# Second pass of a graph kernel: TensorE's results staged by ScalarE and added two experts later, self loops made ahead of the gathers, a written order on four engines

## The chip, the core and the metric

The kernel runs on one core of a Trainium2 chip, as one program. The metric is the time of one execution in microseconds (us) on the device; the smaller, the better. Before the change the median of nine runs is 2969.44 us, and the runs lie between 2944.95 and 2984.15 us.

The core's engines run side by side, each with its own queue, and wait for each other through semaphores. TensorE (PE) multiplies matrices and writes into PSUM, a small memory in banks of 512 floats per partition. VectorE (DVE) and ScalarE (ACT) read PSUM and the larger on-chip memory, SBUF. GpSimd (POOL) issues the indirect transfers here, and SyncE (SP) most of the direct ones.

## The reference

Two layers over 3125 nodes with 256 features and 103125 edges (50000 random pairs in both directions, and a self loop for each node). Cut to what matters:

```
xn = layernorm(x)
x  = x + L0_gnn(xn, src, dst) + L0_mix(xn)             # a maximum over edges, and attention
x  = x + L0_ffn(layernorm(x))                          # two experts for all nodes
xn = layernorm(x)
x  = x + L1_gnn(xn, src, dst, edge_type) + L1_mix(xn)  # a sum over edges by relation, and attention
x  = x + L1_ffn(layernorm(x))                          # eight experts, two weighted by node
```

The change lies in the second layer:

```
# L1_gnn
agg  = segment_sum((xn @ W[r])[src, edge_type], dst)
h    = gelu(agg + xn @ loop_w + h_bias + xn)
gnn  = layernorm(h) * ln_gamma + ln_beta
# L1_ffn, xn now the normalised x
w    = softmax over the two largest of xn @ Wr + br, 0 for the other six experts
y    = sum over e of w[e] * (gelu(xn @ W1[e] + b1[e]) @ W2[e] + b2[e])
```

All eight experts are computed for every node, since the weights differ from node to node.

## The kernel before

Nodes are sorted by the number of their edges and put into 25 tiles of 128 (the last has 53). A tile `t` of the second pass needs `STEPS[t]` gathers: each one fetches, for the 128 nodes, one row of 256 floats of the table `htab` in device memory (`gather`, L193). `edge_pass` (L1334) walks over groups of tiles (`GROUPS1`: first the four tiles 15 to 18, whose gathers start early, then 23 and 24, 19 to 22, 12 to 14, 9 to 11, 7 and 8, 5 and 6, 3 and 4, and 2, 1, 0 alone). Up to four gathers fill one of five `gt` buffers, and VectorE adds them up (L1356) and into the tile's accumulator (L1361), which begins as the row of the tile's self-loop edge.

Everything else of the layer is background work. It stands as a list of jobs with a cost in `bg`. After each buffer of gathers, `edge_pass` takes as many jobs from the list as a credit allows: 0.9 to 1.3 units of cost for each gather, as is left in the list against the gathers left in the group. So the jobs are written between the gather sums, and VectorE and POOL execute them in this written order (`manual_schedule` with these two engines). TensorE and ScalarE get their order from the planner of the language, which sorts by its own estimate of costs. On the chip each engine then runs its queue strictly in the order decided at build time.

When the last tile of a group has its sums, `after1` appends that group's jobs (class `Group`, L2286), which run beside the gathers of the next group:

- `sums_a`, `sums_b`, `sums_c`: TensorE makes the products of the nodes' own rows with `w_lu`, a matrix of two halves (`loop_w` plus the identity, and the attention's matrix), into PSUM (L2300 to L2302). VectorE adds one half to the accumulator (L2307) and the other to `x` (L2308), and ScalarE applies Gelu (L2309).
- `states_a` to `states_d`: two layer norms on VectorE, with three square roots on ScalarE in between.
- `routes_a`, `routes_b`, `shares`: TensorE transposes the normalised rows and makes the router's logits (L2378); VectorE ranks the experts in `top2` (L197), which has one Exp on ScalarE; TensorE transposes the weights, and ScalarE copies them (L2399).
- ten steps (`step`, L2461). `hidden(e)` makes an expert's first products (L2408) into four PSUM banks, and ScalarE's Gelu moves them to SBUF as `hT` (L2412, three buffers). `outputs(e)` makes the second products (L2439) into two more banks, one bank for two tiles. `take` at the beginning of the next step has VectorE multiply each tile's result by its weight and add it to `x`, straight out of PSUM (L2458). `constants` does the same for the biases `b2` (L2425, L2450, L2456).

The last four steps of a group (`late`) are put between the first jobs of the next one. A finished tile is scattered to the output by POOL (L240), nine buffers of gathers after its last step. Before all this the list holds the attention: `att_k`, `att_softmax`, then `att_ctx` (L2241) for each tile, and `att_end`.

Of the kernel before, what the change touches and what calls it, by code (L numbers as in the profile page):

```python
# [32 lines left out]
NX = 8  # L33
# [27 lines left out]
SECONDS = 5  # L61

# [27 lines left out]
def rows(t):  # L90
    return LAST if t == NT - 1 else P
# [9 lines left out]
def gps_kernel(ctx: ExitStack, tc: tile.TileContext, a, out):  # L101
# [1216 lines left out]
    def fast():  # L1318
        fx = ExitStack()
# [245 lines left out]
        with ExitStack() as l0x:  # L1565
# [376 lines left out]
            ET = mybir.EngineType  # L1942
# [216 lines left out]
        with ExitStack() as l1x:  # L2159
# [23 lines left out]
            f1 = l1x.enter_context(tc.tile_pool(name="f1", bufs=3))  # L2183
# [57 lines left out]
            def att_ctx(t):  # L2241
                r = rows(t)
                pt = ps_tr.tile([P, 2, P], F32, name="pt")
                PE.transpose(pt[:r, 0, :], kT[:, t * P : t * P + r], ident)
                ks = kp.tile([P, P], F32, name="ks1", bufs=3)
                S.activation(ks[:r, :], pt[:r, 0, :], AF.Copy, scale=rs2[:r, t : t + 1])
                PE.matmul(pctx, ks[:r, :], x[:r, t, :], start=(t == 0), stop=(t == NT - 1))  # L2247

            def att_sum():
                S.copy(g_t, pctx)  # L2250
# [35 lines left out]
            class Group:  # L2286


                def __init__(self, tiles, accs):
# [3 lines left out]
                    self.hT, self.ys = {}, []  # L2293

                def loops(self, a, b):

                    for j in range(a, min(b, self.k)):
                        pa = self.pa[j] = ps_mm.tile([P, 512], F32, name="mm")
                        at = slice(self.tiles[j] * P, (self.tiles[j] + 1) * P)
                        PE.matmul(pa, xT[:, 0, at], w_lu[:, 0, :], start=True, stop=False)  # L2300
                        PE.matmul(pa[:, :D], ones_row, b_h, start=False, stop=False, skip_group_check=True)  # L2301
                        PE.matmul(pa, xT[:, 1, at], w_lu[:, 1, :], start=False, stop=True)  # L2302

                def gelus(self, a, b):
                    for j in range(a, min(b, self.k)):
                        t, mg, pa = self.tiles[j], self.accs[j], self.pa.pop(j)
                        V.tensor_tensor(mg, mg, pa[:, :D], op=ALU.add)  # L2307
                        V.tensor_tensor(x[:, t, :], x[:, t, :], pa[:, D:], op=ALU.add)  # L2308
                        S.activation(self.hh[:, j, :], mg, AF.Gelu)  # L2309

                def sums_a(self):
                    self.hh = fin.tile([P, 4, D], F32, name="hh")
                    self.mvh = [small.tile([P, 4, 2], F32, name=f"mvh{i}") for i in range(2)]
                    self.rsh = [small.tile([P, 4], F32, name=f"rsh{i}") for i in range(3)]
                    self.pa = {}
                    self.loops(0, 2)

                def sums_b(self):
                    self.gelus(0, 2)
                    self.loops(2, 4)  # L2320

                def sums_c(self):
                    self.gelus(2, 4)
# [41 lines left out]
                def routes_a(self):  # L2365
# [9 lines left out]
                    self.pl = ps_tr.tile([P, 512], F32, name="pt")  # L2375
                    for j, t in enumerate(self.tiles):
                        for c in range(2):
                            PE.matmul(  # L2378
                                self.pl[:, j * NX : (j + 1) * NX], xT[:, c, t * P : (t + 1) * P], wr1[:, c, :],
                                start=(c == 0), stop=(c == 1),  # L2380
                            )

                def routes_b(self):
                    k = self.k
                    lg1 = fin.tile([P, 4, NX], F32, name="lg1")
                    V.tensor_tensor(
                        lg1[:, :k, :], self.pl[:, : k * NX].rearrange("p (j e) -> p j e", e=NX),
                        br1[:, None, :].to_broadcast([P, k, NX]), op=ALU.add,
                    )
                    w_full, _ = top2(lg1[:, :k, :], k, fin)  # L2390
                    V.tensor_copy(wf[:, self.s, :], w_full)

                def shares(self):
# [6 lines left out]
                    self.constants()  # L2400

                def hidden(self, e):
                    n, at0 = self.n, self.at0
                    hT = self.hT[e] = f1.tile([P, FC, 4 * P], F32, name="hT1")
                    for f in range(FC):
                        ph = ps_mm.tile([P, 512], F32, name="mm")
                        for c in range(2):
                            PE.matmul(  # L2408
                                ph[:, :n], w1s[e][:, c, f * P : (f + 1) * P], xT[:, c, at0 : at0 + n],
                                start=(c == 0), stop=(c == 1),  # L2410
                            )
                        S.activation(hT[:, f, :n], ph[:, :n], AF.Gelu, bias=b1[:, e, f : f + 1])  # L2412

                def bank(self):
                    turn[0] += 1
                    return ps_acc.tile([P, 512], F32, name="py", tag=f"acc{1 + turn[0] % 2}")

                def constants(self):

                    for j0 in range(0, self.k, 2):  # L2420
                        pb = self.bank()
                        two = self.tiles[j0 : j0 + 2]
                        for j, t in enumerate(two):
                            r, at = rows(t), (j0 + j) * P
                            PE.matmul(  # L2425
                                pb[:r, j * D : (j + 1) * D], self.wT[:, at : at + r], b2a, start=True, stop=True
                            )
                        self.ys.append((None, two, pb))

                def outputs(self, e):  # L2430

                    hT = self.hT.pop(e)
# [227 lines left out]
```

## Time and profile before

| what | value |
|---|---|
| median of nine runs | 2969.44 us |
| the profiled execution | 2958.72 us |
| its span | 2957.0 us |
| second pass, from its first gather on | 1652 to 2957 us |
| last sum of gathered rows | 2899 us |
| VectorE's busy time in L2458 | 88.1 us, 200 instructions |
| ScalarE's busy time from 1652 us on | 289 us |
| granted TensorE clock, mean | 0.766 |

A row of the groups' view reads: line, engine, operation, output and inputs by the names in the program, shapes, count, then busy time and the mean of one in ns, and after the bar the time in which the engine stood idle just ahead of these instructions, with what ended the waiting. In the view of waits the three numbers are us in total, how often, and the longest. "issue" is time in which the engine waited for nothing that the profile shows. "remote", or "another core or an unknown queue", marks a wait whose releasing event the profile could not name. A matrix product of 32-bit floats shows as two records.

### The profile page before, as it was taken

Reading aid. Unit: us, or ns where it says so; the run is one execution under the profiler, and the core shown is the slowest. Engines: PE = TensorE matmul, PEld = TensorE weight load, DVE = VectorE, ACT = ScalarE, POOL = GpSimd, SP = SyncE. Lnnn points to the kernel's source line nnn. Section 1 sums busy time; section 2 is a strip of 40 time slices with the busy share of each in tenths; the row PEclk is TensorE's granted clock in tenths of the full one; section 3 lists DMA queues with packets and bytes.
Section 4 is the critical chain, followed back from the end, with each engine's and each line's share of the span. In section 5 each row is a group of like instructions: output and inputs, shape, how many; then the busy total and the mean of one; then the engine's idle time right before and its main releaser. Section 6 shows DMA issues by size and latency. Waiting matters only on the chain.

```text
span 2957.0 us, 20996 instructions
## 1 busy us (share of the span) xinstructions
PE 1878.8 (64%) x6033; PEld 1173.0 (40%) x6033; DVE 1256.5 (42%) x3537; ACT 558.5 (19%) x1275; POOL 1727.2 (58%) x1830
## 2 busy tenths in 40 slices
PE   4374666403473754266798447867887787786877
PEld 3132333202341433134443224554455455564656
DVE  7443444536324434324665334334353344343342
ACT  5122221000110101012221112121112121222234
POOL 5566665676647477646026764665666566665561
PEclk9666877655785766567899667887898788887889
DMA  6433333343323233333256642232332223222220
GB/s 190 127 88 88 92 90 95 94 106 111 94 62 106 61 96 95 90 70 81 74 196 227 213 124 64 84 89 81 88 89 84 80 81 86 82 87 83 77 82 16
DMA packets 125963, 290.09 MB, mean 98 GB/s; under 512 B 41387, under 2 KB 63983, under 8 KB 122633
## 3 DMA queue, kind: packets, MB, share of 16 engines
q0 software_dynamic: 83184, 230.02, 28.2%
q1 hardware_dynamic: 38122, 55.88, 5.6%
q10 hardware_dynamic: 4526, 2.71, 0.3%
q8 instruction: 51, 0.84, 0.1%
q14 instruction: 80, 0.65, 0.1%
HBM read 249.07 MB, written 39.41 MB: 98 GB/s over the span
## 4 chain that ended last, share of the span: by engine, by line
PE 27%; issue 8%; another core or an unknown queue 6%; DVE 5%; POOL 3%; ACT 2%; DMA 1%; DVEq 0%; POOLq 0%; ACTq 0%
PE mm L2408 10%; PE py L2439 8%; PE mm L188 4%; POOL gt L193 3%; DVE gt L1356 1%; PE mm L2302 1%; PE pt L2378 1%; DVE bnst L162 1%; PE mm L2300 1%; ACT hT L2412 0%; PE py L2425 0%; PE mm L2301 0%; PE pctx L2247 0%; DMA gt<-htab_f,idx2g 0%
## 5 line engine op out<-in xcount | busy, mean ns | idle before, releaser
L193 POOL DMA_INDIRECT gt<-btab,idx x814 | 804.9, 989 | 476.1 <-issue 225.9
L193 POOL DMA_INDIRECT gt<-htab_f,idx2g x742 | 732.3, 987 | 463.8 <-DVE acc L1361 227.3
L2408 PE MATMUL mm<-xT,w 128*128 128x256 f32 (+4 forms) x1408 | 438.7, 462 | 125.5 <-issue 78.3
L1356 DVE TENSOR_TENSOR gt<-gt 128x256 f32<-128x256 f32 (+1 forms) x767 | 409.9, 534 | 80.7 <-remote 36.6
L2439 PE MATMUL py<-w,hT 128*128 128x256 f32 (+1 forms) x1600 | 395.8, 401 | 58.5 <-issue 28.9
L2408 PEld LDWEIGHTS mm<-xT,w 128*128 128x128 f32 x1408 | 269.6, 219 | 272.1 <-issue 187.5
L2439 PEld LDWEIGHTS py<-w,hT 128*128 128x128 f32 (+1 forms) x1600 | 314.6, 200 | 130.7 <-issue 73.9
L2458 DVE SCALAR_TENSOR_TENSOR x<-py,wf,x 128x256 f32<-128x256 f32 x200 | 88.1, 478 | 484.9 <-remote 204.5
L2412 ACT ACTIVATE hT<-mm,b 128x256 f32<-128x256 f32 (+4 forms) x352 | 168.3, 496 | 569.7 <-PE mm L2408 251.3
L188 PE MATMUL mm<-w_rel,xT 128*128 128x512 f32 x400 | 178.8, 605 | 6.0 <-ACT xT L183 3.9
L1532 PE MATMUL mm<-w,hT 128*128 128x256 f32 x400 | 131.5, 489 | 68.5 <-issue 47.1
L1503 PE MATMUL mm<-xT,w 128*128 128x384 f32 (+2 forms) x320 | 113.9, 522 | 91.6 <-issue 39.0
L1361 DVE TENSOR_TENSOR acc<-acc,gt 128x256 f32<-128x256 f32 x371 | 158.4, 427 | 27.4 <-DVE gt L1356 11.5
L1532 PEld LDWEIGHTS mm<-w,hT 128*128 128x128 f32 x400 | 94.1, 246 | 120.3 <-issue 77.2
L188 PE MATMUL mm<-w_qkv,xT 128*128 128x512 f32 (+1 forms) x200 | 102.0, 633 | 43.4 <-ACT vs L1751 28.1
L1503 PEld LDWEIGHTS mm<-xT,w 128*128 128x128 f32 x320 | 70.1, 244 | 134.3 <-issue 61.1
L188 PE MATMUL pt<-w_own,xT 128*128 128x256 f32 x100 | 39.8, 527 | 123.2 <-DVE acc L1845 69.1
L188 PEld LDWEIGHTS mm<-w_rel,xT 128*128 128x128 f32 x400 | 76.3, 194 | 100.9 <-issue 88.3
L1863 PE MATMUL pmean<-ones,xt 128*128 128x1 f32 (+1 forms) x100 | 21.0, 314 | 130.0 <-DVE xt L171 86.6
L193 POOL DMA_INDIRECT gt<-htab_f,soon x72 | 72.2, 1003 | 46.3 <-issue 20.0
L1620 DVE COPY slots<-gt 128x4 f32<-128x4 f32 (+1 forms) x214 | 38.5, 180 | 134.9 <-DMA gt<-btab,idx 134.5
L1507 ACT ACTIVATE hT<-mm,b 128x384 f32<-128x384 f32 (+2 forms) x80 | 40.3, 517 | 223.6 <-remote 140.8
(436 smaller groups left out, 2088.2 us busy)
## 6 DMA issues: line engine op xcount, KB each, us to landing
htab_f<-hs SPq DMA_DIRECT2D x25, 1024.0 KB
gt<-btab,idx POOLq DMA_INDIRECT x814
gt<-htab_f,idx2g POOLq DMA_INDIRECT x742
w<-in_f_W_dram SPq DMA_DIRECT2D x20, 512.0 KB
ntab<-x SPq DMA_DIRECT2D x5, 640.0 KB
btab<-bs SPq DMA_DIRECT2D x5, 640.0 KB
x<-in_x_dram SPq DMA_DIRECT2D x4, 640.0 KB
otab<-xn SPq DMA_DIRECT2D x16, 128.0 KB
```

What stands on the lines that cost most here:

```text
L188: PE.matmul(ps, lhs[:, c, t * P : (t + 1) * P], w[:, c, :], start=start and c == 0, stop=stop and c == 1)
L193: G.indirect_dma_start(out=dst, out_offset=None, in_=table, in_offset=bass.IndirectOffsetOnAxis(ap=idx, axis=0))
L1356: V.tensor_tensor(gt[:, :h, :], gt[:, :h, :], gt[:, m - h : m, :], op=op)
L1361: V.tensor_tensor(acc, own(t) if i == 0 else acc, gt[:, 0, :], op=op)
L1503: PE.matmul(ph[:, :n], w1[:, i, c, f * P : (f + 1) * P], xT[:, c, at0 : at0 + n], start=(c == 0), stop=(c == 1),)
L1507: S.activation(hT[:, f, :n], ph[:, :n], AF.Gelu, bias=b1[:, i, f : f + 1])
L1532: PE.matmul(py[:, i * D : (i + 1) * D], hTs[i][:, f, j * P : (j + 1) * P], w2[:, i, f, :], start=False, stop=(f == FC - 1), skip_group_che ...
L1620: V.tensor_copy(slots_of[t][:, U - 1 - k1 : U - 1 - k0], gw[:, : k1 - k0, D])
L2408: PE.matmul(ph[:, :n], w1s[e][:, c, f * P : (f + 1) * P], xT[:, c, at0 : at0 + n], start=(c == 0), stop=(c == 1),)
L2412: S.activation(hT[:, f, :n], ph[:, :n], AF.Gelu, bias=b1[:, e, f : f + 1])
L2439: PE.matmul(py[:r, j * D : (j + 1) * D], hT[:, f, at : at + r], w2s[e][:, f, :], start=(f == 0), stop=(f == FC - 1),)
L2458: V.scalar_tensor_tensor(d, y, wf[:r, t, e : e + 1], d, op0=ALU.mult, op1=ALU.add)
```

## The change

The change touches the second pass, the function `fast`.

1. ScalarE and TensorE join the engines with a written order: all four now run the second pass as the jobs write it. The jobs of a group are interleaved by hand with the end of the group before (`group_jobs`, `last_jobs`).
2. `brought` has ScalarE copy each expert's results out of PSUM into one of two `ys` buffers in SBUF, multiplied by the weight. `taken` has VectorE add a whole group's buffer to `x` in one instruction, and it does so as late as the buffers allow: when both are full and a third result is to be staged, the older one is added first.
3. `loops` makes the products with `w_lu` for the next group two steps ahead of the end of this one's jobs, while that group's gathers are still running, and ScalarE copies both halves to SBUF (`hu`). `sums` then adds from SBUF.
4. The router's logits are copied to SBUF by ScalarE, `hT` has two buffers in place of three, and `att_ctx` makes its product after the next tile's transposes (`att_add`).

```diff
+YS = 2
...
-            f1 = l1x.enter_context(tc.tile_pool(name="f1", bufs=3))
+            f1 = l1x.enter_context(tc.tile_pool(name="f1", bufs=2))
...
-                PE.matmul(pctx, ks[:r, :], x[:r, t, :], start=(t == 0), stop=(t == NT - 1))
+                if t:
+                    att_add(t - 1)
...
+                def loops(self):
+                    self.hu = fin.tile([P, 4, 2, D], F32, name="hu")
+                    self.hh = self.hu[:, :, 0, :]
...
+                    for j, (pa, _) in enumerate(pas):
+                        got = S.copy(self.hu[:, j, :, :], pa.rearrange("p (m d) -> p m d", m=2))
+                def sums(self):
...
+                    for j, mg in enumerate(self.accs):
+                        V.tensor_tensor(self.hh[:, j, :], self.hh[:, j, :], mg, op=ALU.add)
+                        S.activation(self.hh[:, j, :], self.hh[:, j, :], AF.Gelu)
+                    V.tensor_tensor(x[:, self.s, :], x[:, self.s, :], self.hu[:, :k, 1, :], op=ALU.add)
...
+                def brought(self, e):
+                    if len(brought) == YS:
+                        taken()
+                    ys = fin.tile([P, 4, D], F32, name="ys", bufs=YS)
...
+                        if e is None:
+                            got = S.copy(ys[:r, j, :], py)
+                        else:
+                            got = S.activation(ys[:r, j, :], py, AF.Copy, scale=wf[:r, t, e : e + 1])
+                    brought.append((self, e, ys))
...
                 def step(self, i):
-                    self.take()
-                    if i < NX:
-                        self.hidden(i)
-                    if 1 <= i <= NX:
-                        self.outputs(i - 1)
...
+                    self.hidden(i)
+                    self.outputs(i - 1 if i else None)
+                    self.gelus(i)
+                    self.brought(i - 1 if i else None)
+            def taken():
+                group, e, ys = brought.popleft()
...
+                    d = x[:, tiles[0] : tiles[0] + k, :]
+                    V.tensor_tensor(d, d, ys[:, :k, :], op=ALU.add)
...
+            def group_jobs(new, old):
+                k, c = new.k, old.k if old else 0
+                out = [(3.0, new.sums)]
+                if old:
+                    out.append((1.5 * c, all_of(
+                        lambda: old.hidden(6), lambda: old.gelus(6), lambda: old.outputs(5), lambda: old.hidden(7),
+                    )))
+                out += [(1.5, new.states_a), (1.5, new.states_b), (1.0, new.states_c)]
+                if old:
+                    out.append((2.0 * c, all_of(
+                        lambda: old.brought(5), lambda: old.gelus(7), lambda: old.outputs(6),
+                    )))
+                out += [(1.0, new.states_d), (4.0, new.routes_a)]
+                if old:
+                    out.append((2.5 * c, all_of(
+                        lambda: old.brought(6), lambda: old.outputs(7), lambda: old.brought(7),
+                    )))
+                out += [(2.0, new.routes_b), (2.0, new.shares)]
+                out += [((1.6 if i == 0 else 3.1) * k, lambda i=i: new.step(i)) for i in range(6)]
+                return out
...
+                jobs = group_jobs(groups1[g], groups1[g - 1] if g else None)
+                if g + 1 < len(GROUPS1):
+                    groups1.append(Group(GROUPS1[g + 1], None))
+                    jobs.insert(len(jobs) - 2, (2.0, groups1[g + 1].loops))
...
-            with tc.manual_schedule(engines={mybir.EngineType.DVE, mybir.EngineType.Pool}):
+            with tc.manual_schedule(engines={ET.DVE, ET.Pool, ET.PE, ET.Activation}):
                 first_group()
```

## The prediction

> **What bounds the kernel now.** I read the page first. No engine is full: POOL, which issues the gathers, is the busiest over the second pass, and the chain that ended last runs through TensorE's two FFN lines.
>
> ```profile
> PE 1878.8 (64%) x6033; PEld 1173.0 (40%) x6033; DVE 1256.5 (42%) x3537; ACT 558.5 (19%) x1275; POOL 1727.2 (58%) x1830
> PE mm L2408 10%; PE py L2439 8%; PE mm L188 4%; POOL gt L193 3%; DVE gt L1356 1%; PE mm L2302 1%; PE pt L2378 1%; DVE bnst L162 1%; PE mm L2300 1%; ACT hT L2412 0%; PE py L2425 0%; PE mm L2301 0%; PE pctx L2247 0%; DMA gt<-htab_f,idx2g 0%
> ```
>
> Next the waits from 1651 us to the end, which is the second pass. VectorE spends 440 us in three rows in front of one line, L2458, the weighted addition out of PSUM. POOL then waits for VectorE, since its gathers need the five `gt` buffers back.
>
> ```profile
> POOL gt L193 <- DVE acc L1361: 227.3, 53, 13.2
> DVE x L2458 <- remote: 204.5, 15, 24.6
> DVE x L2458 <- PE py L2439: 149.5, 50, 20.1
> DVE x L2458 <- PE mm L2408: 85.7, 8, 25.7
> ```
>
> Third, busy time by group of tiles (columns: window, length, then busy PE, PEld, DVE, ACT, POOL). I cut the windows where the gathers of one group end; the cuts are those of the sum below.
>
> ```profile
> 1652.00:1714.00 62.00, 14.79 (x40) 8.22 (x38) 19.54 (x21) 9.84 (x17) 47.98 (x47) 0.56 0.54 167
> 1714.00:1809.00 95.00, 55.97 (x165) 31.04 (x166) 43.24 (x106) 22.84 (x44) 45.76 (x46) 0.73 0.33 96
> 1809.00:1980.00 171.00, 141.46 (x488) 92.48 (x486) 65.94 (x165) 31.90 (x53) 105.24 (x109) 0.85 0.30 85
> 1980.00:2135.00 155.00, 119.61 (x375) 71.47 (x376) 59.83 (x149) 27.83 (x51) 99.77 (x101) 0.80 0.30 88
> 2135.00:2299.00 164.00, 126.79 (x405) 81.66 (x404) 67.09 (x168) 28.11 (x46) 102.22 (x105) 0.83 0.29 86
> 2299.00:2420.00 121.00, 95.82 (x317) 63.91 (x316) 48.08 (x126) 23.14 (x40) 70.84 (x73) 0.84 0.28 80
> 2420.00:2541.00 121.00, 97.42 (x359) 70.03 (x359) 50.21 (x129) 27.95 (x49) 73.77 (x76) 0.87 0.29 82
> 2541.00:2662.00 121.00, 87.48 (x326) 68.35 (x324) 49.50 (x128) 24.59 (x49) 78.30 (x80) 0.82 0.30 86
> 2662.00:2727.00 65.00, 40.09 (x143) 29.96 (x144) 24.58 (x66) 13.46 (x26) 40.47 (x43) 0.77 0.30 85
> 2727.00:2801.00 74.00, 58.92 (x227) 45.38 (x227) 24.89 (x63) 17.85 (x36) 41.37 (x43) 0.89 0.28 79
> 2801.00:2899.00 98.00, 76.58 (x397) 64.12 (x396) 44.95 (x135) 37.20 (x83) 54.60 (x55) 0.87 0.25 73
> ```
>
> The reader is to see that every stretch is longer than its PE time and longer than its POOL time: the two alternate. The cause is a loop. PSUM has two output banks, four tiles fill both, and VectorE frees them by an addition that stands in its queue among the gather sums. TensorE waits for VectorE to come round, then VectorE waits for TensorE.
>
> Last, the timeline, around one 20 us wait:
>
> ```profile
> 1806.89 7.07 PE L2439 MATMUL py<-w,hT 128*128 128x256 f32 x32
> ...
> 1874.52 4.70 PE L2439 MATMUL py<-w,hT 128*128 128x256 f32 x21
> 1876.62 0.95 POOL L193 DMA_INDIRECT gt<-htab_f,idx2g  x1 [0.30 <-issue]
> 1882.54 1.29 PE L2439 MATMUL py<-w,hT 128*128 128x256 f32 x2 [1.73 <-issue]
> 1885.34 0.58 PE L2439 MATMUL py<-w,hT 128*128 128x256 f32 x1 [1.51 <-issue]
> 1895.31 1.66 DVE L2458 SCALAR_TENSOR_TENSOR x<-py,wf,x 128x256 f32<-128x256 f32 x4 [20.15 <-PE py L2439]
> ```
>
> The same 32 products took 7.07 us at 1807 and 20 us at 1875, with nothing awaited ("issue"). TensorE has slow stretches of its own, and the change doesn't touch them.
>
> **The change part by part.**
>
> *Additions staged (L2412 to L2459).* VectorE loses 200 L2458 instructions at 478 ns (88 us of busy time on the page), 14 of L2450 (8.1) and 2 of L2456 (0.7): 97 us. It gains nine additions for each of eleven groups. Priced by SBUF rows of the same width, 426 ns at 256, 685 at 512, 1.22 us at 1024 and about 0.95 between for 768, a round over all groups is 3 x 0.43 + 4 x 0.69 + 2 x 0.95 + 2 x 1.22 = 8.4 us, so 76, and 4 for the short last tile. 17 us of VectorE saved, beside gathers and off the path. What counts is its 440 us of waiting. An expert's result is now added two steps after it is staged; a four-tile step of TensorE takes 7.0 (L2408 x16) + 7.07 (L2439 x32) = 14 us, so VectorE may run some 28 us ahead before it waits: longer than any single wait above (25.7).
>
> ScalarE gains 200 scaled evictions of 128x256; the nearest row is its own Gelu of that shape, 472 ns (copies without a scale 373): 94 us, plus 25 constants at 373 ns (9). ScalarE then works some 400 us of 1150, and a four-tile step has 4 x 0.69 + 4 x 0.47 = 4.6 us of it under 14 us of TensorE. It is hidden as long as VectorE hands back one of the two `ys` buffers; a late VectorE holds the eviction, the next Gelus queued behind it, and so TensorE.
>
> The Trainium skill ("ScalarE: Activation LUTs", Rules for kernel authors) speaks against this: additions and multiplications belong on VectorE. The rows put the two engines level here, 478 ns against 472; by the rule up to 94 us would come back (2934 in the end), by the trace none, since they lie under TensorE's work.
>
> *Self loops ahead (L2295 to L2309).* TensorE's products stay (50 each of L2300, L2301, L2302). Moved ahead, they take away VectorE's wait at L2307 (55.1 + 4.8 us). ScalarE gains 25 copies of 128x512 at 590 ns (15 us), behind TensorE. VectorE loses 50 PSUM additions at 415 ns (21 us) and gains 25 at 427 plus one wide addition a group: 10.7 + 8.4 = 19. Level.
>
> *`hT` buffers three to two.* Nothing: on a TensorE in program order the products that read a buffer are over before the Gelus that refill it can start.
>
> *`att_ctx`.* The product moves behind the next transposes. Its wait for ScalarE is 14.5 us in all, in stretches where VectorE waits for gathers anyway: between 0 and -14, I take 0.
>
> *Table loads.* ScalarE made 56 in this pass at 1283 ns. The written order needs about four a switch, 43: -17 us of ScalarE, hidden; 0.
>
> *Queues passed.* Expert loads and `otab` loads on SP keep their place among the gathers. Scatters on POOL (1021 ns each) are released by the last addition, two steps later, and POOL's wait for it is bounded by the nine chunks kept in between, so 0; past the last gather nothing is behind them but the end.
>
> *Fixed order on TensorE and ScalarE.* This is the cost. At each of ten group switches: `hidden(0)` of the new group now stands behind the transposes of the routing weights. Before, it ran while VectorE ranked experts (7.79 us from 1789.85, beside ranking from 1790.04 to 1795.3). Transposes and logits wait on VectorE and ScalarE with nothing between, some 2.5 us. And the Exp stands on ScalarE behind the evictions of experts 6 and 7. Lower bound 0 (VectorE's pace by gathers is slower than TensorE anyway), upper bound 7.8 + 2.5 + 7 (one `outputs`) = 17 us a switch. I take 8, nearer the first, since most stretches have TensorE time to spare.
>
> **The sum.** A gather takes 0.95 + 0.30 us when POOL waits for nothing (the row at 1876.62). By stretch the larger of gathers x 1.25 and today's busy PE: 58 (46 gathers), 58 (46), 141 (PE), 120 (PE), 127 (PE), 96 (PE), 97 (PE), 97 (77 gathers), 51 (41), 59 (PE), 77 (PE), and the 58 us tail as it is: 1039 us, where 1305 were spent. That is 266 us to win at most. Back come 10 x 8 = 80 us of switches, and part of TensorE's own delays: VectorE's "remote" waits of 204.5 us were moments in which TensorE's results came late. Bounds 0 (all absorbed by the 28 us of slack) and 204; slack hides them from VectorE but TensorE and ScalarE still pay in the stretches where PE is the larger, so I take 60. Gain 266 - 80 - 60 = 126 us. The profiled execution took 2958.7 us, so 2833; the median of the runs lies 10.7 us above it: about 2843, said as 2840.
>
> The page counts 51 packets of the instruction queue q8 for 12066 PE instructions and weight loads, 16.5 KB and some 237 instructions each. The Trainium skill ("Runtime: NRT & Kernel Launch", Instruction fetch mechanics) says that code comes in 16 KiB blocks of 256 instructions and that crossing one is mostly hidden. By that rule the slow stretch at 1875 would not be the fetch and the 60 us would be 0; the trace shows the slowness, whatever its cause, and the sum goes by it.
>
> **The rivals.**
>
> *All of it is won.* The slack absorbs switches and late results: 2969 - 266 = 2703, with half the switches 2743. For it: 28 us exceeds each wait. Against it: in six stretches TensorE is already the longer side, and it must also meet its partners in order.
>
> *TensorE simply is the bound.* If its "remote" and slow time all comes back (204) together with a switch cost of 6 us, the gain is gone: 2969 - 266 + 204 + 60 = 2967, no change. For it: 1809 to 1980, PE 83% busy with few waits on VectorE. Against it: the 155 us and 164 us stretches with 36 us of idle PE each.
>
> *Slower: the strict order closes a new loop at the switches.* VectorE needs the Exp, the Exp stands behind the evictions of experts 6 and 7, those need `outputs(7)`, which stands behind transposes that need VectorE; gathers stop with VectorE once the five buffers are full. It decides from 27 us a switch (266 / 10); at 32 us the time is 3020. For it: TensorE's lag of up to two steps (28 us) must be worked off just there. Against it: 17 us was the worst I could add up, and one round of the old loop cost 20 to 25 us too.
>
> **How the numbers follow.** Forecast (2780 to 2900): 0.47. All won (2690 to 2780): 0.18. No change, or nearly (2900 to 2985): 0.17, of it 0.07 below 2954. Slower by the loop: 0.18. About 0.5% (15 us) is what a measurement of this kernel can tell from no change. So faster 0.47 + 0.18 + 0.07 = 0.72, same 0.10, slower 0.18. The range leaves out a tenth at each end: 2715 to 3000.
>
> **What will show it.** Right: VectorE's waits on TensorE at the additions fall from 440 us to under 100, POOL's wait for VectorE at L193 from 227 to under 110, second-pass PE idle from about 350 us to 220, ScalarE to about 400 us busy. Wrong: a new top wait, VectorE on ScalarE (the Exp in `top2` or the Sqrt in `root`) above 150 us in all, or TensorE idle above 15 us at each switch. The forecast fails high if TensorE's slow stretches grow as it gets denser, and low if they vanish.

## The result and the profile after

| | before | after |
|---|---|---|
| median of the runs (62 and 20) | 2959.94 us | 3029.97 us |
| ratio after / before, 95% interval | | 1.0206 [1.018, 1.0232] |
| second pass in the profiled execution | 1305 us | 1408 us |
| TensorE busy in it | 958 us | 968 us |
| VectorE waiting in front of the experts' additions | 440 us | 303 us (L2474) |
| all waits of POOL for VectorE in it | 303 us | 397 us |

The changed kernel is 2.1% slower. The ratio leaves out the runs that lie over 1.5% above the fastest of their kernel; the medians of all runs give 2.4%. The readings of "after" are taken from a run of the unaltered changed kernel that was made beside the first experiments (profiled execution: 3057.7 us, 28 above the median; span 3056.0 us, second pass from 1648 us). The page's engine row and its chain by line answer the two shown before:

```profile
PE 1890.0 (62%) x6033; PEld 1183.6 (39%) x6033; DVE 1235.8 (40%) x3415; ACT 649.8 (21%) x1525; POOL 1733.8 (57%) x1830
...
PE mm L2402 11%; PE py L2430 9%; PE mm L190 5%; DVE gt L1359 1%; ACT hT L2412 1%; PE mm L2315 1%; PE mm L2313 1%; ACT ys L2447 1%; PE mm L2214 0%; PE pctx L2256 0%; PE py L2428 0%; DVE bnst L164 0%; PE mm L2314 0%; DVE x L2346 0%
```

The work went where the change puts it: VectorE has 122 instructions less, ScalarE 250 more and 91 us more to do. TensorE's work is the same. The waits of the second pass (us in total, times, longest):

```profile
POOL gt L195 <- DVE acc L1364: 260.9, 34, 38.0
DVE x L2474 <- ACT ys L2447: 230.7, 27, 27.4
...
DVE bnst L164 <- ACT hu L2325: 187.1, 9, 41.6
...
ACT hT L2412 <- remote: 138.0, 29, 10.5
ACT ys L2447 <- remote: 122.9, 10, 26.7
...
DVE x L2474 <- ACT ys L2445: 72.6, 6, 24.6
...
DVE t_w L219 <- ACT t_w L216: 57.5, 7, 21.0
```

VectorE still waits 303 us at the additions (L2474), now for ScalarE's staged results in place of TensorE's PSUM; the whole idle time in front of the line is 392, where it was 485. Two waits stand beside that: 187 us for the Gelu of new sums (L2325; `bnst` is the first operation of the norm behind it), where before has no such row, and 58 us for the ranking's Exp (L216), which was 35. ScalarE itself waits in rows that end in "remote": the product that it needs is over in TensorE's records, and the signal comes later. By group, in the same cut as before (window, length, busy PE, PEld, DVE, ACT, POOL, then granted clock, DMA share, GB/s):

```profile
1813.00:2005.00 192.00, 143.75 (x492) 93.69 (x490) 62.66 (x139) 47.20 (x93) 106.22 (x107) 0.85 0.26 75
...
2169.00:2340.00 171.00, 114.47 (x361) 71.80 (x361) 56.76 (x130) 38.79 (x74) 102.19 (x105) 0.79 0.28 83
2340.00:2480.00 140.00, 107.67 (x337) 69.44 (x337) 48.67 (x115) 38.88 (x77) 70.33 (x72) 0.84 0.24 69
...
2740.00:2819.00 79.00, 52.33 (x178) 40.22 (x178) 28.59 (x78) 21.70 (x46) 41.56 (x43) 0.74 0.24 70
```

These stretches took 171, 164, 121 and 65 us before. All are longer now, with as many gathers in them, and none is filled by TensorE or POOL. One group switch in the timeline shows how these waits hang together:

```profile
2366.19 1.12 PE L2315 MATMUL mm<-w_lu,xT 128*128 128x512 f32 x2
...
2373.77 0.95 POOL L195 DMA_INDIRECT gt<-htab_f,idx2g  x1 [0.30 <-issue]
2374.69 0.59 ACT L2317 COPY hu<-mm 128x512 f32<-128x512 f32 x1 [9.29 <-remote]
...
2375.30 0.42 DVE L2324 TENSOR_TENSOR hu<-hu,acc 128x256 f32<-128x256 f32 x1 [9.05 <-issue]
...
2375.32 2.45 PE L2402 MATMUL mm<-xT,w 128*128 128x384 f32 x4 [4.14 <-issue]
...
2385.93 0.67 PE L2430 MATMUL py<-w,hT 128*128 128x256 f32 x1 [1.03 <-issue]
...
2387.36 1.52 ACT L2412 ACTIVATE hT<-mm,b 128x384 f32<-128x384 f32 x3 [3.57 <-remote]
...
2401.64 1.01 ACT L2325 ACTIVATE hu<-hu 128x256 f32<-128x256 f32 x3
2402.08 0.43 DVE L164 BATCH_NORM_STATS2 bnst<-hu 128x6 f32<-128x256 f32 x1 [23.90 <-ACT hu L2325]
...
2406.07 0.94 POOL L195 DMA_INDIRECT gt<-htab_f,idx2g  x1 [22.39 <-DVE acc L1364]
```

The self-loop product ends at 2367.3, and ScalarE goes on 7 us later (2374.69), while POOL issues a gather every 1.25 us (until 2383.7). TensorE then waits four and one us for nothing that is shown. The sums are complete at 2375.7, but their Gelus, 1.0 us of work for three tiles, start at 2401.64: they are queued behind the old group's Gelus and evictions, and those behind TensorE. VectorE stands 23.9 us in front of them, and POOL, for want of a free `gt` buffer, 22.4.

That pause also shows TensorE with and without gathers (columns as above):

```profile
2375.00:2393.00 18.00, 14.20 (x36) 9.23 (x37) 2.80 (x5) 4.05 (x9) 6.82 (x7) 0.72 0.20 59
2393.00:2411.00 18.00, 18.00 (x73) 13.50 (x72) 5.78 (x18) 7.75 (x15) 3.79 (x4) 1.00 0.08 23
```

In the first 18 us, with gathers until 2383.7, TensorE does 36 matmul records; in the next 18, with gathers only from 2406 on, 73 without a gap.

### The profile page after: what moved, and what is told of

Read it like the earlier page. It is cut to its first block, busy times and chain, and to the rows that moved or that the text cites. A ratio compares the mean times of both kernels' runs of the same rounds, so it can differ in the third digit from the quotient of the medians.

```text
span 3051.1 us, 21182 instructions
## 1 busy us (share of the span) xinstructions
PE 1905.6 (62%) x6033; PEld 1189.7 (39%) x6033; DVE 1233.5 (40%) x3415; ACT 648.7 (21%) x1525; POOL 1729.1 (57%) x1830
## 4 chain that ended last, share of the span: by engine, by line
PE 29%; issue 9%; another core or an unknown queue 6%; DVE 3%; ACT 3%; POOL 1%; DMA 1%; ACTq 0%; DVEq 0%; POOLq 0%; SPq 0%
PE mm L2402 11%; PE py L2430 10%; PE mm L190 4%; POOL gt L195 1%; PE mm L2315 1%; ACT ys L2447 1%; PE mm L2313 1%; ACT hT L2412 1%; DVE gt L1359 1%; DMA gt<-htab_f,idx2g 0%; PE py L2428 0%; PE mm L2314 0%; PE pt L2381 0%; PE pctx L2256 0%
## 5 line engine op out<-in xcount | busy, mean ns | idle before, releaser
L195 POOL DMA_INDIRECT gt<-btab,idx x814 | 799.7, 982 | 481.7 <-issue 224.4
L195 POOL DMA_INDIRECT gt<-htab_f,idx2g x742 | 739.8, 997 | 551.2 <-DVE acc L1364 247.1
L2402 PE MATMUL mm<-xT,w 128*128 128x256 f32 (+4 forms) x1408 | 415.6, 451 | 112.6 <-issue 76.4
L2430 PE MATMUL py<-w,hT 128*128 128x256 f32 (+1 forms) x1600 | 418.6, 414 | 97.7 <-issue 87.3
L2430 PEld LDWEIGHTS py<-w,hT 128*128 128x128 f32 (+1 forms) x1600 | 326.6, 207 | 176.0 <-issue 111.2
L2474 DVE TENSOR_TENSOR x<-x,ys 128x256 f32<-128x256 f32 (+3 forms) x99 | 73.1, 739 | 400.0 <-ACT ys L2447 234.9
L2447 ACT ACTIVATE ys<-py,wf 128x256 f32<-128x256 f32 x200 | 84.5, 473 | 338.6 <-remote 121.7
L190 PE MATMUL pt<-w_own,xT 128*128 128x256 f32 x100 | 41.5, 542 | 108.8 <-remote 73.1
L195 POOL DMA_INDIRECT gt<-htab_f,soon x72 | 72.2, 1002 | 46.5 <-issue 19.6
```

The lines of the kernel that those rows point to most:

```text
L190: PE.matmul(ps, lhs[:, c, t * P : (t + 1) * P], w[:, c, :], start=start and c == 0, stop=stop and c == 1)
L195: G.indirect_dma_start(out=dst, out_offset=None, in_=table, in_offset=bass.IndirectOffsetOnAxis(ap=idx, axis=0))
L2402: end = PE.matmul(ph[:, :n], w1s[e][:, c, f * P : (f + 1) * P], xT[:, c, at0 : at0 + n], start=(c == 0), stop=(c == 1),)
L2430: end = PE.matmul(py, hT[:, f, at : at + r], w2s[e][:, f, :], start=(f == 0), stop=(f == FC - 1))
L2447: got = S.activation(ys[:r, j, :], py, AF.Copy, scale=wf[:r, t, e : e + 1])
L2474: V.tensor_tensor(d, d, ys[:, :k, :], op=ALU.add)
```

## The theories

**Theory 1**: the order written by hand for ScalarE or TensorE closes a loop at the group switches (the prediction's slower rival). **Theory 2**: TensorE sets the pace, with delays of its own that the gathers cause; taking VectorE out of its way wins nothing. **Theory 3**: the additional step through ScalarE costs by itself, whatever the order.

The runs were made on several chips. On all but one the kernel before takes 2960 to 2982 us; the exception has a section of its own. Ratios are always to runs of the kernel before on the same chip.

## Experiments on the order

**The changed kernel again**, no edit.

> The changed kernel once more, unaltered, for a profile beside the runs that follow on the same chip. All theories: 3010 to 3050 us, a ratio near 1.02.

Measured 3052.11 us, ratio 1.0265 [1.0197, 1.0332]; a third time, on another chip and beside the later runs:

> The changed kernel, unaltered, as the measure for the other three of this call. On a chip where the kernel before takes about 2965 us: 3030 to 3060 us, ratio 1.02 to 1.03. On a chip where it takes about 2477 us (TensorE undisturbed, the gathers' issuing the pace): theory 2 has nothing to win or lose there, ratio 1.000 to 1.006; if the written order costs by itself whatever the chip (theory 1), 1.02 or more there too.

Measured 3052.12 us, ratio 1.0232 [1.0165, 1.0298].

**TensorE and ScalarE back to the planner, all else as changed.**

```diff
-            with tc.manual_schedule(engines={ET.DVE, ET.Pool, ET.PE, ET.Activation}):
+            with tc.manual_schedule(engines={ET.DVE, ET.Pool}):
                 first_group()
```

> The changed kernel, with TensorE and ScalarE ordered by the planner again in the second pass; staging, self loops ahead and the order of the jobs stay. Theory 1 (the written order is the loss: at each switch the Gelu of the new sums stands on ScalarE behind the old group's Gelus and evictions, and VectorE with the gathers waits for it): 2880 to 2960, VectorE's wait for that Gelu below 80 us from 187. Theory 2 (TensorE is the bound in both kernels, and slow stretches of its own decide): 2940 to 3000, the waits move to other lines. Theory 3 (the extra step through ScalarE is the loss, whatever the order): 3000 to 3050.

Measured 2962.64 us, ratio 0.9964 [0.9918, 1.001]. So the staging, the early self loops and the second trip through ScalarE together are worth nothing that can be told from zero, and cost nothing: theory 3 falls. The loss lies in the order. VectorE's waits at the additions are 345 us here in place of 440, those for the square roots 110 in place of 6, and the time stays: less waiting at the additions alone doesn't shorten the pass.

**The kernel before with its own job order written out for TensorE and ScalarE too.**

```diff
-            with tc.manual_schedule(engines={mybir.EngineType.DVE, mybir.EngineType.Pool}):
+            with tc.manual_schedule(engines={ET.DVE, ET.Pool, ET.PE, ET.Activation}):
```

> The kernel before, with TensorE and ScalarE in the order in which its jobs are written in the second pass, and nothing else. Theory 1: slower by more than the change, 3030 to 3150, since its jobs were not laid out for it. Theory 2: 2960 to 3030. Theory 3: within 1% of 2960, since no staging is added.

Measured 2978.59 us, ratio 1.0028 [0.9991, 1.0065]. Theory 1 had asked for 3030 or more. A written order as such costs next to nothing in the kernel before; what costs is the written order of the changed jobs (`group_jobs`, with the staging).

**Only ScalarE's order to the planner** (the set without `ET.Activation`), and its mirror, **only TensorE's** (without `ET.PE`).

> ScalarE's order in the second pass left to the planner, the other three written by hand. On a chip of 2965 us, theory 1 in its narrow form (ScalarE's order costs it): 2950 to 2985 us, VectorE's wait for the Gelu of the sums under 60 us. Rival (TensorE's order): 3030 to 3060 us. On a chip of 2477 us: 2487 again.

> TensorE's order in the second pass left to the planner, ScalarE's written by hand with VectorE's and GpSimd's. On a chip of 2965 us: ratio 1.015 to 1.03 if the cost is ScalarE's order (theory 1 in its narrow form), 0.995 to 1.01 if it is TensorE's order, or if either alone suffices. On a chip of 2477 us: 1.003 again.

Measured 2994.88 us, ratio 1.0061 [1.0036, 1.0086], for ScalarE planned, beside 3052.12 for the changed kernel on the same chip; and 3036.12 us, ratio 1.0172 [1.0074, 1.027], for TensorE planned. The first number lies between the ranges that were expected. The waits in the changed kernel on that chip, then with ScalarE planned:

```profile
DVE x L2474 <- ACT ys L2447: 251.4, 31, 27.6
...
DVE bnst L164 <- ACT hu L2325: 197.5, 9, 36.4
...
DVE t_w L219 <- ACT t_w L216: 78.1, 10, 20.2
```

```profile
DVE x L2474 <- ACT ys L2447: 376.5, 41, 30.8
POOL gt L195 <- DVE acc L1364: 235.8, 34, 22.4
...
DVE rsh L2356 <- ACT rsh L2330: 75.6, 8, 25.5
...
DVE t_w L219 <- ACT t_w L216: 4.6, 6, 3.6
...
DVE bnst L164 <- ACT hu L2325: 0.2, 1, 0.2
```

The two waits that theory 1 names went from 197.5 and 78.1 us to 0.2 and 4.6. Most of that came back elsewhere: 125 us more in the first row at the additions (103 in both of the line's rows for ScalarE), 74 more in front of a square root. Net, VectorE's waiting fell by 75 us, POOL's for VectorE by 59, and the time by 57. ScalarE's order is worth 1.7 of the 2.3%; with TensorE planned the wait for the Gelu stays (192.3 us), and the time does not differ beyond its interval. With both planned the ratio was 0.9964, and its interval ends below that of ScalarE planned alone: by these runs TensorE's order costs about 1% once ScalarE's is out of the way.

**The first hidden products ahead of the ranking.**

```diff
-                    self.hidden(i)
+                    if i:
+                        self.hidden(i)
...
-                out += [(2.0, new.routes_b), (2.0, new.shares)]
+                out += [(2.0, all_of(lambda: new.hidden(0), new.routes_b)), (2.0, new.shares)]
```

> The new group's first hidden products issued ahead of its ranking on VectorE. On a chip of 2965 us: 2970 to 2990 us if TensorE's wait behind the ranking (priced at 7.8 us a switch) is on the path, 3030 to 3065 us if not. On a chip of 2477 us: 2487 again.

Measured 3061.79 us, ratio 1.0246 [1.0167, 1.0326], beside 1.0232. TensorE's place behind the ranking, the largest single piece of the prediction's price for a switch, is worth nothing that can be told; its 7.8 us a switch would have been 60 to 80.

**The norm's jobs later, behind `brought(5)`, `gelus(7)` and `outputs(6)`.**

```diff
-                out += [(1.5, new.states_a), (1.5, new.states_b), (1.0, new.states_c)]
                 if old:
                     out.append((2.0 * c, all_of(
                         lambda: old.brought(5), lambda: old.gelus(7), lambda: old.outputs(6),
                     )))
+                out += [(1.5, new.states_a), (1.5, new.states_b), (1.0, new.states_c)]
```

> The changed kernel with the first layer norm of a new group moved behind the second part of the old group's last experts, so that VectorE comes to the Gelu of the sums some 8 units of cost later. Theory 1 (the place where VectorE meets ScalarE at a switch costs the time): the wait of 187 us for that Gelu falls by over 100 and the time to 2960 to 3010. Theory 2 (TensorE lags, and VectorE must wait somewhere): the wait shows up at the next meeting (additions from ys, the square roots, the Exp), time 3020 to 3070.

Measured 3082.32 us, ratio 1.0385 [1.0278, 1.0492]. VectorE's wait for the Gelu fell from 187 to 69 us, that for the first square root rose from 34 to 131, and that for the staged results from 231 to 355. The kernel is slower still, above both ranges that were expected. Giving VectorE other work in front of the wait only moves it to VectorE's next meeting with ScalarE.

## Experiments on TensorE's pace

**A quarter of the gathers**: one for each buffer of four, and no adding within the buffer. In the changed kernel and in the kernel before:

```diff
-                        for k in range(k0, k1):
+                        if own is not None:
+                            m, k0_ = 1, k1 - 1
+                        else:
+                            k0_ = k0
+                        for k in range(k0_, k1):
```

> The changed kernel with one gather for each buffer of up to four in the second pass, and no additions within a buffer; sums over edges are left out, the order and pace of the jobs stay. POOL and VectorE then have far less to do. Theory 2 in its strict form (TensorE alone sets the pace): 2900 to 3030, TensorE's waits stay. If TensorE is slow because of the gathers' traffic: 2700 to 2850, with its stretches of 0.7 us steps gone. Theory 1 and 3: below 2850 too, as VectorE's waits at the switches cost nothing once the gathers are few, but with the slow stretches still there.

> The kernel before with one gather per buffer in the second pass and no adding within the buffer (three quarters of the gathered rows are left out of the sums). The changed kernel with the same cut took 2657 us. If the decoupling of VectorE was a real gain that only TensorE's disturbance swallows (the prediction's loop through the two output banks): 2700 us or more. If the staging is worth nothing even without the disturbance (TensorE's products are the pace then, whoever reads them): 2640 to 2680 us. On a chip where the kernel before takes 2477 us neither can be told from the number.

Measured 2656.84 us for the changed kernel, 2608.55 for the one before, one run each and on two chips. The first lies below the 2700 to 2850 us that were expected if the gathers slow TensorE, the second below both of its ranges. Of 742 gathers 228 are left, since those of the first group stay. TensorE's delays are gone with the gathers. In the changed kernel the whole view of the second pass has 20.5 us of "remote" waits, against 394 with all gathers, and TensorE's matmuls start after 46 us of "issue", against 207. What is left there:

```profile
DVE x L2478 <- ACT ys L2451: 222.8, 37, 12.1
ACT ys L2451 <- PE py L2434: 213.9, 90, 5.1
DVE bnst L164 <- ACT hu L2329: 151.6, 10, 26.0
```

Here TensorE is 86% busy (865 us of the 1003 from 1652 us to the end), and the changed kernel is 48 us behind the kernel before: with TensorE the pace, the change as it stands has nothing to give. Whether the 48 us are its order, at 5 us a switch, no run shows.

**All gathers issued, a quarter added** (`m = 1` with the loop over the gathers as it was).

> All gathers of the second pass issued, one of each buffer added (three quarters of the gathered rows are left out of the sums), as in the run with 2474 us on the chip where the kernel before takes 2477. On a chip of 2965 us, theory 2 (the gathers themselves slow TensorE): 2930 to 3050 us, gaps without a wait 80 us or more. Rival (it was VectorE's adding and what waits for it): 2660 to 2780 us. On a chip of 2477 us: 2474 again.

Measured 3049.71 us, beside 3052.12 for the changed kernel on the same chip. VectorE is some 190 us less busy than in the changed kernel, and the time does not move: it is the gathers themselves, not the adding of their rows, that cost the 390 us of the last comparison. The late signals are back:

```profile
ACT ys L2449 <- remote: 212.4, 20, 23.2
...
DVE bnst L164 <- ACT hu L2327: 196.0, 9, 35.9
ACT hT L2414 <- remote: 138.5, 27, 11.3
```

**A quarter of the bytes**: as many gathers, each with rows of 64 floats in place of 256, and additions as narrow; three quarters of each row are left out.

```diff
+        h_short = htab.rearrange("n (r d) -> (n r) d", d=D // 4)
...
-                            gather(gw[:, k1 - 1 - k, :], table, ids[:, U - 2 - k : U - 1 - k])
+                            gather(gw[:, k1 - 1 - k, :], h_short if own is not None else table, ids[:, U - 2 - k : U - 1 - k])
```

> The changed kernel with the gathers of edge_pass in the second pass as many as before, but of 64 floats in place of 256 (and additions of that width): POOL issues as many transfers and descriptors, a quarter of the bytes; the sums are not the reference's. If bytes in flight slow TensorE: 2650 to 2850, as with a quarter of the gathers, the 0.7 us steps gone. If the number of transfers, or POOL's issuing, slows it: 2950 to 3060, with the steps.

Measured 3044.97 us, 1.021 of the kernel before beside it (2981.31), as the changed kernel. By this one run, what slows TensorE goes with the number of gathers (or of the rows that they fetch), not with their bytes.

**Half of the second products** (two of four parts of `hT`), and **the hidden products in two column halves** (the same arithmetic in 1408 more matmul records and as many weight loads):

```diff
-                        for f in range(FC if e is not None else 0):
+                        for f in range(2 if e is not None else 0):
...
```

```diff
-                        for c in range(2):
-                            end = PE.matmul(
-                                ph[:, :n], w1s[e][:, c, f * P : (f + 1) * P], xT[:, c, at0 : at0 + n],
+                        for lo, hi in ((0, n // 2), (n // 2, n)):
+                            for c in range(2):
+                                end = PE.matmul(
+                                    ph[:, lo:hi], w1s[e][:, c, f * P : (f + 1) * P], xT[:, c, at0 + lo : at0 + hi],
```

> The changed kernel with half of the second expert products left out (two of four parts of the hidden layer). TensorE loses 800 products of about 216 ns, 173 us. Theory 2 (TensorE sets the pace nearly throughout): 2850 or less, at least its 173 us gone. Theory 1 (latencies between engines at the switches set it): 2950 to 3020.

> The changed kernel with each first expert product cut into two halves of its columns: the same arithmetic, 1408 products and as many weight loads more on TensorE in the second pass. If the supply of TensorE's instructions is what runs slow among the gathers: 3120 or more (11 more blocks of 256 instructions at about 10 us), with more idle time put down to issue. If the array or its data are slow: within 40 us of the changed kernel.

Measured 2957.09 us (0.992 of the kernel before beside it, 93 to 103 us less than the changed kernel by its two ratios) for 158 us of TensorE's busy time taken away, with "remote" waits of 412 us, as many as ever; and 3168.44 us (1.063, 108 to 118 us more) for 83 us of busy time added. The second fits theory 2, whose delays go with the number of TensorE's instructions, but 83 of these us are TensorE's own longer work, so it is weak evidence. In the first, some three fifths of the 158 us came back: TensorE's amount of work is on the path in part, but less than theory 2 asked for (2850 us or less), and its lateness stays.

## The other chip

Four kernels happened to run on a chip on which the kernel before takes 2477 us, 16% less than on the others.

> The changed kernel with the order written by hand on VectorE, GpSimd and TensorE in the second pass, and ScalarE's left to the planner. Theory 1 in its narrow form (what the written order costs is ScalarE's: the Gelu of new sums stands behind the old group's Gelus and evictions): back to the planner's time, 2950 to 2985 us, and VectorE's 187 us of waiting for that Gelu falls under 60. Rival (it is TensorE's order, no product can be taken ahead): stays at 3030 to 3060 us. If each bears a part: about 3000 us.

> The mirror of the last one: the order written by hand on VectorE, GpSimd and ScalarE, TensorE's left to the planner. Theory 1 in its narrow form: stays at 3030 to 3060 us, with VectorE's wait for the Gelu of the sums at 150 us or more. Rival (TensorE's order): 2950 to 2985 us.

> The changed kernel with the new group's first hidden products issued ahead of its ranking on VectorE instead of behind the transposed shares. The prediction priced TensorE's wait behind the ranking at 7.8 us of the 8 us a switch, ten switches. If that is on the path: 60 to 80 us less, 2970 to 2990 us. If TensorE's place at the switch is not what sets the pace (theory 2, or ScalarE's order alone): within 15 us of the changed kernel, 3030 to 3065 us.

> The changed kernel with every gather of the second pass issued as before, into the same buffers, but with only the first row block of each buffer added: three quarters of the gathered rows are left out of the sums, as in the run with a quarter of the gathers, which took 2657 us. VectorE does the same little work as there; only the transfers are back. Theory 2 (the gathers themselves slow TensorE's supply of instructions and the arrival of its results): most of the 390 us come back, 2930 to 3050 us, and TensorE's gaps without a wait are back from 6 us to 80 or more. Rival (what the quarter saved was VectorE's adding and what waits for it): 2660 to 2780 us.

Measured 2486.86 us (1.0039 [1.0026, 1.0053]), 2484.91 (1.0031 [1.002, 1.0042]), 2486.68 (1.0031 [1.0017, 1.0045]) and 2473.87 us. All the numbers that were expected are missed, since none of them thought of such a chip. The part ahead of the second pass is shorter there too: its first gather starts at 1416 us, in place of 1648. One kernel on both chips, the one with ScalarE planned, shows what differs. On the faster chip, the gathers' group row in the second pass (after the bar the idle time and its causes):

```profile
L195 POOL DMA_INDIRECT gt<-htab_f,idx2g x742 | 745.2, 1004 | 240.1 <-issue 201.7 <-DVE acc L1364 12.6 <-DVE rsh L2363 5.4
```

then the stretch of tiles 19 to 22, with the columns of the groups' view above, and the longest row of its waits:

```profile
1552.00:1691.00 139.00, 133.71 (x500) 91.01 (x501) 65.87 (x144) 50.24 (x101) 106.58 (x107) 0.98 0.37 103
```

```profile
DVE gt L1359 <- DMA gt<-htab_f,idx2g: 322.1, 117, 5.5
```

The same group row and the same stretch on a chip of 2982 us:

```profile
L195 POOL DMA_INDIRECT gt<-htab_f,idx2g x742 | 739.2, 996 | 497.2 <-DVE acc L1364 235.8 <-issue 203.0 <-DVE sums L2116 22.9
```

```profile
1816.00:2000.00 184.00, 143.87 (x493) 91.81 (x492) 62.80 (x139) 47.58 (x95) 105.64 (x106) 0.86 0.27 77
```

The gathers take the same time to issue (1004 and 996 ns), VectorE and ScalarE are as busy, but the stretch takes 139 us in place of 184. In the second pass there isn't one wait that ends in "remote" (452 us on the chip of 2982), and no matmul starts after an "issue" wait (265 us). POOL waits 55 us in all for VectorE, in place of 333, and VectorE waits for gathers, as it should where these are the pace. The second pass takes 1072 us, with 742 gathers that need 947 us to issue. TensorE's own busy time in the pass is 853 us in place of 945, with a granted clock of 0.89 in place of 0.80; that is a third of the difference between the passes (1072 and 1338 us), and in the rest TensorE stands idle. The three kernels that compute the whole result are 0.3 to 0.4% slower than before there. So nothing was won where there is no lateness to absorb; but all three keep the written order on TensorE or on ScalarE, and the version with both planned didn't run there.

## Why the prediction was wrong

Predicted were 2840 us and a range from 2715 to 3000; 3030 were measured.

**What held.** VectorE's additions: 80 us priced, 77 measured (73.1 in L2474, 3.8 in L2477), for the 97 of before. ScalarE's evictions: 94 + 9 us priced, 84.8 + 8.2 measured; 25 copies of 15 us, 14.6; ScalarE busy some 400 us, 378 measured. The scaled copy on ScalarE is indeed level with VectorE's weighted addition (473 and 478 ns) and hidden: the run with both orders planned shows no cost of it, so the weighing against the rule of the Trainium skill ("ScalarE: Activation LUTs", Rules for kernel authors) came out as the trace said, not as the rule does. The 1039 us that the sum of the larger engine gave as the least time of the pass is near what an undisturbed chip takes (1072, with ScalarE planned).

**Two misreadings.** POOL isn't the busiest engine of the second pass before: TensorE is, with 958 us against 762. And the sum itself has TensorE as the longer side in seven stretches, not six. Both speak for the rival that TensorE is the bound.

**The step that failed: the gain itself.** The reading said that the two engines alternate, and that the cause is a loop through two output banks which VectorE frees. The alternation is there; the cause is not. TensorE's own waits in the kernel before show it:

```profile
PE mm L2408 <- issue: 78.3, 53, 7.0
...
PE py L2439 <- DVE x L2458: 21.5, 3, 14.8
```

Of its 347 us of idle time 153 are "issue", 98 waits for ScalarE and 85 waits for VectorE, and of these only 21.5, in three places, are second products that wait for the additions that free the banks. The half of the loop in which TensorE waits for VectorE to come round is small. TensorE's results and instructions come late while gathers are issued: three quarters fewer gathers, or a chip without the effect, and the lateness is gone, and with the gathers back but not added it is back. So most of the 266 us between the pass and its least time went with the disturbance, and buffers between TensorE and VectorE didn't win them. Measured, the change without its order gave 0.4% by its ratio (2962.64 for 2964.7 beside it, not told from zero) where the sum had 206 us (266 - 60). The term "TensorE's late results", taken as 60 between 0 and 204, was in truth nearly the whole of the 266. I read it so, though no run shows it by itself: 28 us of slack hide a single late result, but the results are late again and again, and the slack is used up and never refilled. The longest wait at the additions is still 27 us.

**The waits that should go.** VectorE's at the additions fell to 303 us, not under 100; POOL's at L195 rose from 227 to 261, not under 110; TensorE's idle time in the pass went from 347 to 440 us, not to 220. The self loops' wait of 60 us, which I took as removed, is 68 us now in front of L2324 (43.1 "issue", 24.5 for ScalarE's copy): ahead of time in the jobs, the product is still late.

**The order.** 10 x 8 = 80 us was the right size, by luck: leaving ScalarE's order to the planner gives back 57 us, both orders some 80 to 90 (1.0232 or 1.0265 against 0.9964). It is made of other things than those priced. `hidden(0)` behind the ranking, 7.8 us a switch, is nothing that can be told. The Exp behind evictions is real, some 20 to 40 us more waiting in all. The largest, the Gelu of the new sums behind the old group's Gelus and evictions, the price doesn't have, although the jobs show it: `sums` stands behind `step(4)` and `step(5)` of the old group. When VectorE reaches it, TensorE lags, and ScalarE has eight Gelus and six evictions of these steps to do first (2383 to 2401.6 us in the timeline above).

**The rivals.** "TensorE simply is the bound" (0.17, 2967 us) had the mechanism of what was not won. The slower rival had the place of the loss, ScalarE at the switches, and missed its price: it asked for 27 us a switch because it had 266 us of gain to eat first. With no gain, 6 to 9 us a switch were enough to be slower. Put together by the runs, the profiled 2958.7 + 10.7, less some 10 for the change without its order, and 57 to 90 for the order come to 3016 to 3049.

**The supply of code.** I set the lateness against the Trainium skill's "Runtime: NRT & Kernel Launch" (Instruction fetch mechanics), by which crossing a block of code is mostly hidden. That the 60 us would then be 0 doesn't follow: another cause costs as much. The runs show that the delay goes with the number of gathers and differs between chips, and not by which way TensorE is delayed; whether the supply of its code is part of it stays open.

**What stays open.** Why gathers delay TensorE on most of the chips and not on one; how the unaltered change and the trace of before look on that chip, where only altered versions ran; whether TensorE's lower granted clock is a part of the cause or comes of the waiting; and whether more `ys` buffers would help, which wasn't tried. No version was shown to beat the kernel before: the best, both orders planned, has an interval that takes in 1.

## What to carry to other kernels

Idle time on both sides of a hand-over is a gain only if a buffer can move the work; before pricing it, look whether the late side is late by itself ("remote" and "issue" rows, products that take three times as long with nothing awaited), and treat that part as lost until a run without the suspected neighbour says otherwise. A loop has two halves: before calling it one, read how long the late side waits for the other (here 21.5 us). A written order for an engine that serves two groups must be read from that engine's side: list what stands in front of each short operation that another engine stops for. And a rival that must first eat a gain is priced against the chance that there is no gain.

## What the runs showed of the hardware

- On all chips of these runs but one, indirect gathers slow TensorE, which they don't use: with all of them in the pass, ScalarE and VectorE spend 366 to 588 us in "remote" waits, with 228 of them 20 to 28 us. A quarter of their bytes changes nothing (467 us).
- The delay is a matter of the chip: the same kernel takes 2487 us on one and 2995 on another, with the same time for each gather (1004 and 996 ns), as much busy time on VectorE (497 and 492 us in the pass) and ScalarE (409 on both), and with no "remote" wait on the faster one.
- TensorE's granted clock goes with its lateness: 0.98 in the stretch of tiles 19 to 22 on the faster chip, 0.86 on the other; 1.00 in the 18 us without a gap shown above, 0.72 in the 18 before. Which follows from which isn't shown.
